# A four-layer graph network: 0/1 matrices kept in DRAM from layer 0 to layer 2, and two additions moved to other layers

## The chip, the cores and the metric

The kernel runs on one core of a Trainium2 chip. Times are device microseconds (us) of that core for one execution. The time before is 5064.37 us, the median of three runs (5048.0 to 5065.55).

Engines: PE (matrix multiplication; PEld is its weight load, which overlaps it), DVE (vector engine), ACT (scalar engine), POOL (GpSimd) and SP (SyncE, which only issues DMAs here). Each engine works through its own instructions in a fixed order. DMAs are issued from the queues of SP, ACT and POOL; the indirect ones, gathers and scatters with a row address per partition, are POOL's.

## The reference

50,000 nodes with 64 features, 25,000 directed edges that come sorted by their destination. Four layers, each with a normalisation and a rectification ahead of it and a residual sum behind it:

```python
h = maximum(layernorm(x), 0);  x = x + L0(h)    # mean of relu([h[src], h[dst]] @ W_msg + b_msg) over a node's edges,
                                                # then relu([h, mean] @ W_upd + b_upd)
h = maximum(layernorm(x), 0);  x = x + L1(h)    # (h + sum of h[src] * norm over a node's edges) @ W.T + b
h = maximum(layernorm(x), 0);  x = x + L2(h)    # attention over a node's edges (4 heads, 8 edge types),
                                                # y = layernorm(h + attention) * g1 + b1
                                                # L2 = layernorm(y + ffn(y)) * g2 + b2, ffn with gelu
h = maximum(layernorm(x), 0);  x = x + L3(h)    # expm(-t * B) h by a Taylor series of sparse products, B from edge_weight
```

So the x behind layer 2 is `x2 + layernorm(...) * g2 + b2`, where `x2` is the x behind layer 1, and the result is `x + L3(h)` with `L3(h) = h + POLY[1] * (B h) + ...`: the program folds the sub-steps of the series into one polynomial in B, `POLY`.

## The kernel before

**Tiling.** The nodes are taken in 49 items q of 1024 nodes, which lie as 8 blocks of 128 on the partitions (a tile [128, 8, 64]). The edges of an item fill up to 640 slots, 5 slot tiles of 128. As the edges are sorted, a node block j can touch only the slot tiles that the constant `BT[j]` names (first tile, number of tiles), and a slot tile i only the node blocks of `TB[i]`; `OHW` holds the column at which slot tile i begins in a row of 1920 columns.

**0/1 matrices.** A sum over the edges of a node, or the spreading of a node's row to its edge slots, is a matmul with a 0/1 matrix in bf16. There are two of an item. `noh` (node on the partition, slot on the free side; `node_hot`, L1883) is built by 8 DVE comparisons of 128 or 256 columns between the slots' keys, which `load_keys` (L1878) has broadcast to all partitions by a 160 KB DMA, and the node's own number. `soh` (slot on the partition, node on the free side; `slot_hot`, L1891) is built by 5 DVE comparisons of 256 to 512 columns, from a constant row and one key per partition. Layer 0 uses `noh` and `soh`, layer 1 `soh`, layer 2 both; layer 3's first product uses a `soh` with other keys (`skey`, the edges sorted by source). In layers 0 to 2 the keys, and so the matrices, are the same.

**Stages.** Each layer is a list of stages per item, run as a software pipeline: in each step every item in flight does its next stage, and a new item is begun (`Steps` and `pipeline`, L70 to L110). After every stage a hook, `lists_pace`, puts in some instructions of an independent job, building the lists of paths that layer 3's higher powers of B need; these are POOL scatters and gathers (`nmap`, `lgot`, `lrow`) and small DVE, PE and ACT work. Its rate is a number for each layer. From this program order a scheduler makes the fixed order of each engine; the number of buffers of a tile (`bufs`, otherwise 2) says when a buffer can be written again.

- *Layer 0* (L1977 to L2043): `fetch` (5 gathers `ga`, loads of `bt`, `cat`, `xt`, keys), `hots` (`node_hot`, `slot_hot`), `message` (PE with `noh`, then DVE and ACT), `sums` (PE with `soh`), `update`, `project` (stores `x1tab`, `g1tab`).
- *Layer 1* (L2046 to L2101): `fetch`, `scaled` (`slot_hot`, ACT scales the gathered rows), `sums` (L2070: PE into `po`, then DVE `x2 = x1 + po` at L2076, ACT's queue stores `x2tab` at L2077, then norm and rectification), `turn`, `product` (kv, q, h2 to DRAM).
- *Layer 2* (L2104 to L2398) has two pipelines. `up` is `fetch` (L2220: 5 gathers `kvg`, loads of `qt`, keys, `typ`), `hots` (L2231: `types` and `node_hot`), `logits` (L2236: PE `pv`, DVE `kk` and `vv`, store of `vv`, PE `pe` with `noh`). `down` is `fetch2` (L2305: loads of `vv`, `h2`), `message` (L2311: `slot_hot`, then `m3`), `sums` (PE with `soh`), `attend`, `turn`, `close` (loads `x2`), `product`, `finish` (L2370). The items go in batches of 13, 12, 12 and 12, with a softmax at the end of each: first `up` alone for 13 items, then `up` beside `down`, then `down` alone. `finish` multiplies by the norm and by g2 (L2380), adds b2 to `x2` (L2381), adds both (L2382), makes the next `h`, stores it (`h3tab`, L2385), adds it to x (L2386) and stores that (`xstab`, L2387).
- *Layer 3, first product B h* (L2483 to L2512): `fetch` (5 gathers `y` of `h3tab`, load of `xs`), `scaled` (`slot_hot`, ACT's scaling, a split in three bf16 parts), `sums` (PE `po`, ACT `f`, DVE `xs += POLY[1] * f`, stores). Then the higher powers, with final scatters that add to the output.

Of the kernel before, what the change touches and what calls it, by code (L numbers as in the profile page):

```python
# [22 lines left out]
F32 = mybir.dt.float32  # L23
# [35 lines left out]
TB = ((0, 3), (1, 3), (3, 3), (4, 4), (6, 2))  # L59
GRP = ((0, 1), (1, 2), (3, 1), (4, 2), (6, 2))  # L60
OHW = (0, 384, 768, 1152, 1664, 1920)

POLY = np.ones(1)
for _ in range(N_SUB):
# [901 lines left out]
def fast(ctx: ExitStack, tc: tile.TileContext, a: dict, out: bass.AP, flag: bass.AP):  # L966
# [25 lines left out]
    ktab = dram.tile([NQ, RW], F16, name="ktab")  # L992
    ttab = dram.tile([NQ, RW], F16, name="ttab")
    otab = dram.tile([NN, 1], I32, name="otab")
    vvtab = dram.tile([NQ * P, 5 * D], F32, name="vvtab")
    stab = dram.tile([P * TL, PW], I32, name="stab")
    nmap = dram.tile([NN, 1], I32, name="nmap")
# [3 lines left out]
    def nodes(tab, q):  # L1001
        return tab.rearrange("(p b) d -> p b d", p=P)[:, 8 * q:8 * q + 8, :]
# [879 lines left out]

    def node_hot(pool, s):  # L1883

        s.noh = pool.tile([P, 8, 2 * P], BF16, name="noh")
        for j in range(8):
            t0, n = BT[j]
            nc.vector.tensor_scalar(s.noh[:, j, :n * P], s.keys[:, t0 * P:(t0 + n) * P], pblk[:, j:j + 1], None,
                                    op0=OP.is_equal)

    def slot_hot(pool, keys, q):  # L1891
# [8 lines left out]
    def to_slots(po, s, tab, start=True):  # L1900

        for i in range(5):
            b0, nb = TB[i]
            for j in range(b0, b0 + nb):
                c = (i - BT[j][0]) * P
                for k in range(3):
                    nc.tensor.matmul(po[:, i, :], s.noh[:, j, c:c + P], tab[:, j, k * D:k * D + D],
                                     start=(start and j == b0 and k == 0), stop=(j == b0 + nb - 1 and k == 2))

    def to_sums(pa, oh, msg):  # L1910
# [66 lines left out]
    with tc.tile_pool(name="l0c", bufs=1) as cp, tc.tile_pool(name="l0", bufs=2) as pool, \  # L1977
            tc.tile_pool(name="pl0", bufs=1, space=PSUM) as ps:
        wupd = halves(None, a["L0_gnn_W_upd"][D:2 * D, :], a["L0_gnn_W_upd"][0:D, :], cp, "wupd")
        bupd = bias_rows(cp, row_bcast("L0_gnn_b_upd", pool=cp), "bupd")  # L1980
        w1t = cp.tile([P, D], F32, name="w1t")
        for h in range(2):
            nc.scalar.dma_start(w1t[h * D:(h + 1) * D, :], a["L1_gnn_WT"])

        def fetch(q, s):
            s.ga = pool.tile([P, 5, D], F32, name="ga", bufs=4)
            for i in range(5):
                gather(s.ga[:, i, :], atab, nrs[:, q, i:i + 1])
            s.bt = pool.tile([P, 8, BW], BF16, name="bt", bufs=4)
            nc.sync.dma_start(s.bt, nodes(btab, q))  # L1990
            s.cat = pool.tile([P, 2, 512], F32, name="cat", bufs=5)
            load_turned(s.cat, h0t, q)
            s.xt = pool.tile([P, 8, D], F32, name="xt", bufs=6)
            load_x(s.xt, q)
            load_keys(pool, q, s)

        def hots(q, s):
            node_hot(pool, s)
            s.soh = slot_hot(pool, key, q)

        def message(q, s):
            pe = ps.tile([P, 5, D], F32, name="pe", bufs=2)
            to_slots(pe, s, s.bt)
            z = pool.tile([P, 5, D], F32, name="z")
            nc.vector.tensor_add(z, s.ga, pe)
            m3 = pool.tile([P, 5, 3, D], F32, name="m3")
            for i in range(5):
                nc.scalar.activation(m3[:, i, 0, :], z[:, i, :], AF.Relu, scale=cinv[:, q, i:i + 1])  # L2008
            s.parts = split(m3)

        def sums(q, s):
            pa = ps.tile([P, 512], F32, name="pa")
            to_sums(pa, s.soh, s.parts)
            for h in range(2):
                r = slice(h * D, h * D + D)
                nc.scalar.activation(s.cat[r, h, :], pa[r, :], AF.Copy)

        def update(q, s):
            po = ps.tile([P, 8, D], F32, name="po")
            bias_in(po.rearrange("p b d -> p (b d)"), bupd)  # L2020
            for j in range(8):
                nc.tensor.matmul(po[:, j, :], s.cat[:, j // 4, j % 4 * P:j % 4 * P + P], wupd[j // 4],
                                 start=False, stop=(j == 7))
            s.x1 = pool.tile([P, 8, D], F32, name="x1", bufs=3)
            nc.vector.scalar_tensor_tensor(s.x1, po, 0.0, s.xt, op0=OP.max, op1=OP.add)
            s.h = pool.tile([P, 8, D], F32, name="h")
            norm_relu(pool, s.h, s.x1)

        def project(q, s):
            tr = turned(pool, ps, s.h, "pt")  # L2030
            g = pool.tile([P, 8, D], F32, name="g")
            for h in range(2):
                r = slice(h * D, h * D + D)
                pw = ps.tile([P, 4, D], F32, name=f"pw{h}")
                for i in range(4):
                    nc.tensor.matmul(pw[:, i, :], tr[r, i, :], w1t[r, :], start=True, stop=True)
                nc.vector.tensor_add(s.x1[:, h::2, :], s.x1[:, h::2, :], pw)
                nc.vector.tensor_mul(g[:, h::2, :], pw, over(disn[:, 8 * q + h:8 * q + 8:2], 4))
            nc.scalar.dma_start(nodes(x1tab, q), s.x1)
            nc.sync.dma_start(nodes(g1tab, q), g)  # L2040

        lists_pace.rate = 0.5
        pipeline(range(NQ), (fetch, hots, message, sums, update, project), lists_pace)  # L2043

    with tc.tile_pool(name="l1c", bufs=1) as cp, tc.tile_pool(name="l1", bufs=2) as pool, \
            tc.tile_pool(name="pl1", bufs=1, space=PSUM) as ps:
        b1l = bias_rows(cp, row_bcast("L1_gnn_b", pool=cp), "b1l")
        wkv = cp.tile([P, 4 * D], F32, name="wkv")  # L2050
        cen = ident_less_mean(cp)
        for h in range(2):
# [18 lines left out]
        def sums(q, s):  # L2071
            po = ps.tile([P, 8, D], F32, name="po")
            bias_in(po.rearrange("p b d -> p (b d)"), b1l)
            to_nodes(po, s.soh, s.parts, started=True)
            x2 = pool.tile([P, 8, D], F32, name="x2")
            nc.vector.tensor_add(x2, s.x1, po)  # L2076
            nc.scalar.dma_start(nodes(x2tab, q), x2)  # L2077
            s.h2 = pool.tile([P, 8, D], F32, name="h2")
            norm_relu(pool, s.h2, x2)

# [25 lines left out]
    with tc.tile_pool(name="l2c", bufs=1) as cp, tc.tile_pool(name="l2", bufs=2) as pool, \  # L2106
# [103 lines left out]
        pb = ps.tile([P, 1], F32, name="pe")  # L2210
        nc.tensor.matmul(pb, cen, zb[:, 0:1], start=True, stop=True)
        nc.vector.tensor_copy(zb[:, 1:2], pb)
        g2n, b2n = row_bcast("L2_gnn_ln2_g", pool=cp), row_bcast("L2_gnn_ln2_b", pool=cp)

        batches = [(0, 13), (13, 12), (25, 12), (37, 12)]
        batch_of = {q: k for k, (q0, n) in enumerate(batches) for q in range(q0, q0 + n)}
# [4 lines left out]
        def fetch(q, s):  # L2221
# [2 lines left out]
                gather(s.kv[:, i, :], kvtab, nrs[:, q, i:i + 1])  # L2224
            s.qt = pool.tile([P, 8, 3, D], BF16, name="qt", bufs=3)
            nc.sync.dma_start(s.qt.rearrange("p b k d -> p b (k d)"), nodes(qtab, q))
            load_keys(pool, q, s)
            s.typ = pool.tile([NE3, RW], F16, name="typ", bufs=2)
            nc.sync.dma_start(s.typ, ttab[q:q + 1, :].to_broadcast([NE3, RW]))

        def hots(q, s):  # L2231
            s.types = pool.tile([NE3, RW], BF16, name="types")
            nc.vector.tensor_scalar(s.types, s.typ, typei, None, op0=OP.is_equal)
            node_hot(pool, s)

        def logits(q, s):  # L2236
            k = batch_of[q]
# [17 lines left out]
            for i in range(5):  # L2255
                nc.tensor.matmul(pe[:, i, :], s.types[:, i * P:(i + 1) * P], etab[:, KW:], start=True, stop=False)
                b0, nb = TB[i]
                for j in range(b0, b0 + nb):
                    c = (i - BT[j][0]) * P
                    for k in range(3):  # L2260
                        nc.tensor.matmul(pe[:, i, :], s.noh[:, j, c:c + P], s.qt[:, j, k, :], start=False,  # L2261
                                         stop=(j == b0 + nb - 1 and k == 2))
            nc.vector.tensor_mul(kk, kk, pe)
            nc.vector.tensor_reduce(lg, kk.rearrange("p t (h d) -> p t h d", h=NH), AX.X, OP.add)
# [40 lines left out]
        def fetch2(q, s):  # L2305
            s.vv = pool.tile([P, 5, D], F32, name="vv2", bufs=3)
            nc.sync.dma_start(s.vv.rearrange("p t d -> p (t d)"), vvtab[P * q:P * q + P, :])
            s.h2 = pool.tile([P, 8, D], F32, name="h2", bufs=3)
            nc.sync.dma_start(s.h2, nodes(h2tab, q))

        def message(q, s):  # L2311
            k = batch_of[q]
            c = (q - batches[k][0]) * NH
            s.soh = slot_hot(pool, key, q)
            m3 = pool.tile([P, 5, 3, D], F32, name="m3")
            nc.vector.tensor_mul(
                m3[:, :, 0, :].rearrange("p t (h d) -> p t h d", h=NH), s.vv.rearrange("p t (h d) -> p t h d", h=NH),
# [52 lines left out]
        def finish(q, s):  # L2370
# [7 lines left out]
            nc.vector.tensor_mul(halved(x3), po,  # L2378
                                 r.rearrange("p (i h) -> p i h", h=2)[:, :, :, None].to_broadcast([P, 4, 2, D]))
            nc.vector.tensor_mul(x3, x3, along(g2n, 8))  # L2380
            nc.vector.tensor_add(s.x2, s.x2, along(b2n, 8))  # L2381
            nc.vector.tensor_add(x3, x3, s.x2)  # L2382
            h = pool.tile([P, 8, D], F32, name="h")
            norm_relu(pool, h, x3)
            nc.scalar.dma_start(nodes(h3tab, q), h)  # L2385
            nc.vector.tensor_add(x3, x3, h)  # L2386
            nc.scalar.dma_start(nodes(xstab, q), x3)  # L2387

        lists_pace.rate = 1.2
# [93 lines left out]
    with tc.tile_pool(name="mps", bufs=1, space=PSUM) as mps, tc.tile_pool(name="l3", bufs=2) as pool, tc.tile_pool(name="pl3", bufs=2, space=PSUM) as ps:  # L2483
        def fetch(q, s):
# [2 lines left out]
                gather(s.y[:, i, :], h3tab, sptr[:, 5 * q + i:5 * q + i + 1])  # L2487
            s.xs = pool.tile([P, 8, D], F32, name="xs", bufs=4)
            nc.sync.dma_start(s.xs, nodes(xstab, q))

        def scaled(q, s):
            s.soh = slot_hot(pool, skey.rearrange("p (q i) -> p q i", i=5), q)
            y3 = pool.tile([P, 5, 3, D], F32, name="y3")
            for i in range(5):
                nc.scalar.activation(y3[:, i, 0, :], s.y[:, i, :], AF.Copy, scale=swgt[:, 5 * q + i:5 * q + i + 1])
# [129 lines left out]
```

## Time and profile before

| | us |
|---|---|
| median of three runs | 5064.37 |
| the profiled execution | 5101.1 |
| its span, first to last record | 5099.3 |
| PE busy | 2720.2 (53%) |
| DVE busy | 2666.0 (52%) |
| POOL busy | 2207.3 (43%) |
| PEld busy | 1907.3 (37%) |
| ACT busy | 1256.2 (25%) |
| layer 0, from 1096 to 1905 | 809 |
| layer 1, from 1905 to 2610 | 705 |
| layer 2, from 2610 to 3981 | 1371 |
| layer 3's first product, from 3981 to 4420 | 439 |
| the higher powers, to the end | 679 |

Before layer 0 stand the sorting of the edges and the tables, 1096 us in all. The stage borders are read from the first and last records of each layer's tiles; stages overlap a little, as the next layer's first items begin before the last ones of the layer before are done.

How to read the lines that follow in the prediction. A row of the windows view is a stretch of the span: its length, busy us and instructions of PE, PEld, DVE, ACT and POOL, the mean granted clock of PE as a share of full speed, the busy share of the 16 DMA engines, and GB/s. A row of the waits view says: engine, tile and line that waited, what for, us in total, times, longest. A row of the groups view says: line, engine, operation, out<-in with shapes and types, count | busy us, mean ns of one | idle us of the engine just before them, and what ended it ("issue" is no wait that the profile shows, "remote" one whose end it can't place). A row of the timeline is start, length, engine, line, instruction, and in brackets the idle time before it. A row of the DMA queues is packets, MB, and the time of the packets as a share of 16 engines' span; q1 holds SP's, q10 ACT's transfers.

### The profile page before, as it was taken

The numbers are of one execution on the slowest core, as the hardware profiler recorded it, in microseconds if no ns is written. First come the engines' busy times: TensorE is split into PE (matmuls) and PEld (weight loads), VectorE is DVE, ScalarE is ACT, GpSimd is POOL, SyncE is SP. The second block draws the span as 40 slices with busy tenths as digits, with TensorE's granted clock in tenths as the row PEclk, the third lists the DMA queues.
The fourth block names the chain that finished last, engine by engine and source line by source line (L and its number), as shares of the span: only waits on it lengthen the run. The fifth ranks groups of instructions, "written<-read, shape, count | busy, mean of one in ns | idle before, by whom it ended". The sixth has DMA issues, their size and how long they took to land. (4 is left out here: it accounts for less than half of the span.)

```text
span 5099.3 us, 60799 instructions
## 1 busy us (share of the span) xinstructions
PE 2720.2 (53%) x20407; PEld 1907.3 (37%) x20407; DVE 2666.0 (52%) x8592; ACT 1256.2 (25%) x2922; POOL 2207.3 (43%) x2095
## 2 busy tenths in 40 slices
PE   8217304738888984245545763655667354433500
PEld 3002203636667763134433432333333243333400
DVE  9317406866667774245565674566688453312300
ACT  0000103612222223235530332333448222100000
POOL 0770571023323315644425254554320465546786
PEclk9555555556556656567765766767778675555555
DMA  1000214735434424245554222223222344312222
GB/s 38 4 1 2 56 27 130 219 87 140 108 99 110 125 72 110 70 117 167 167 147 118 84 69 72 83 73 88 77 71 82 80 103 119 91 18 41 36 17 12
DMA packets 521881, 424.60 MB, mean 83 GB/s; under 512 B 293924, under 2 KB 400579, under 8 KB 521301
## 3 DMA queue, kind: packets, MB, share of 16 engines
q1 hardware_dynamic: 347236, 241.04, 17.7%
q10 hardware_dynamic: 86976, 126.75, 7.1%
q0 software_dynamic: 87344, 52.82, 6.8%
q8 instruction: 163, 2.67, 0.2%
q14 instruction: 162, 1.32, 0.1%
HBM read 204.24 MB, written 218.11 MB: 83 GB/s over the span
## 5 line engine op out<-in xcount | busy, mean ns | idle before, releaser
L1005 POOL DMA_INDIRECT ga<-atab,nrs x245 | 254.3, 1038 | 773.2 <-DVE bupd_w L1106 304.0
L1936 PEld LDWEIGHTS <-soh 128*128 128x128 bf16 x4410 | 242.5, 120 | 597.7 <-issue 576.0
L1005 POOL DMA_INDIRECT kvg<-kvtab,nrs x245 | 251.4, 1026 | 485.2 <-DVE vv L2251 334.0
L1005 POOL DMA_INDIRECT gt<-g1tab,nrs x245 | 243.6, 994 | 372.5 <-ACT g L2068 213.4
L1005 POOL DMA_INDIRECT y<-h3tab,sptr x245 | 252.2, 1029 | 333.3 <-DVE soh L1896 165.1
L2558 POOL DMA_INDIRECT out<-y,lnode x183 | 283.3, 1548 | 141.3 <-DVE y L2544 75.0
L1926 PE MATMUL pa<-soh,m 128*64 128x256 bf16 (+1 forms) x2646 | 286.1, 338 | 15.6 <-ACT m L2008 11.1
L1188 PE MATMUL pab<-wab,tr 64*128 64x128 f32 x784 | 150.3, 437 | 264.8 <-issue 220.9
L1010 POOL DMA_INDIRECT stab<-raw,pf x196 | 194.6, 993 | 213.4 <-DVE pf L1393 154.0
L1005 POOL DMA_INDIRECT raw<-otab,nrd x196 | 189.9, 969 | 192.3 <-DVE bad L1151 132.5
L2532 DVE TENSOR_SCALAR s<-kr,lkey,lw 128x128 f32<-128x128 f32 x305 | 101.6, 402 | 312.9 <-issue 129.5
L1936 PE MATMUL po<-y,soh 128*128 128x64 bf16 x2205 | 147.3, 225 | 211.5 <-issue 129.4
L1936 PE MATMUL po<-g,soh 128*128 128x64 bf16 x2205 | 142.5, 229 | 208.5 <-DVE ln_v L1130 88.6
L1188 PEld LDWEIGHTS pab<-wab,tr 64*128 64x128 f32 x784 | 136.3, 324 | 283.8 <-issue 223.3
L2537 PE MATMUL pu<-y,s 128*128 128x64 f32 x366 | 109.2, 416 | 245.9 <-issue 99.4
L1130 DVE TENSOR_REDUCE ln_v<-ln_sq 128x8 f32<-128x512 f32 x294 | 196.7, 679 | 81.1 <-ACT ln_sq L1143 55.1
L2261 PE MATMUL pe<-qt,noh 128*128 128x64 bf16 x2205 | 168.9, 225 | 98.5 <-issue 94.1
L1374 DVE SCALAR_TENSOR_TENSOR junk<-rowi,f_sblk,pz 128x392 f32<-128x392 f32 x196 | 114.5, 619 | 196.5 <-remote 118.5
L1926 PEld LDWEIGHTS <-m 128*64 128x64 bf16 x2646 | 183.1, 143 | 91.0 <-issue 45.1
L1896 DVE TENSOR_SCALAR soh<-it,key 128x384 bf16<-128x384 f16 (+2 forms) x735 | 203.8, 316 | 7.9 <-PE pa L1926 3.5
L1005 POOL DMA_INDIRECT lgot<-nmap,ldst x183 | 179.1, 979 | 63.1 <-issue 53.6
L2261 PEld LDWEIGHTS <-noh 128*128 128x128 bf16 x2205 | 117.5, 115 | 212.6 <-issue 127.3
(571 smaller groups left out, 7621.4 us busy)
## 6 DMA issues: line engine op xcount, KB each, us to landing
kvtab<-kv SPq DMA_DIRECT2D x49, 512.0 KB
xt<-in_x SPq DMA_DIRECT2D x96, 256.0 KB
btab<-bt ACTq DMA_DIRECT2D x49, 384.0 KB
bt<-btab SPq DMA_DIRECT2D x49, 384.0 KB
qtab<-qt ACTq DMA_DIRECT2D x49, 384.0 KB
qt<-qtab SPq DMA_DIRECT2D x49, 384.0 KB
keys<-ktab SPq DMA_DIRECT2D x98, 160.0 KB
h0t<-tr ACTq DMA_DIRECT2D x98, 128.0 KB
```

Source lines behind the costliest of these rows:

```text
L1005: return nc.gpsimd.indirect_dma_start(out=dst, out_offset=None, in_=tab[:, :], in_offset=IndirectOffsetOnAxis(ap=idx, axis=0))
L1010: return nc.gpsimd.indirect_dma_start(out=tab[:, :], out_offset=IndirectOffsetOnAxis(ap=idx, axis=0), in_=src, in_offset=None, bounds_chec ...
L1130: nc.vector.tensor_reduce(v, sq, AX.X, OP.add)
L1188: nc.tensor.matmul(pab[:, i, :], s.tr[r, i, :], wab[r, :], start=True, stop=True)
L1374: nc.vector.scalar_tensor_tensor(junk, rowi[:, :BK], sblk[:, t:t + 1], pz, op0=OP.is_equal, op1=OP.mult, accum_out=slot[:, t:t + 1])
L1896: nc.vector.tensor_scalar(oh[:, OHW[i]:OHW[i + 1]], it16[:, b0 * P:(b0 + n) * P], keys[:, q, i:i + 1], None, op0=OP.is_equal)
L1926: nc.tensor.matmul(o, l, r, start=first, stop=last)
L1936: nc.tensor.matmul(po[:, j, :], oh[:, c:c + P], msg[:, i, k, :], start=(not started and i == t0 and k == 0), stop=(end and (not started or ...
L2261: nc.tensor.matmul(pe[:, i, :], s.noh[:, j, c:c + P], s.qt[:, j, k, :], start=False, stop=(j == b0 + nb - 1 and k == 2))
L2532: nc.vector.tensor_scalar(d[:, i, :], kr[:, i, :], s.key[:, t:t + 1], s.w[:, t:t + 1], op0=OP.is_equal, op1=OP.mult)
L2537: nc.tensor.matmul(pu[:, i, :], s0[:, i, :], y[:, t, :], start=True, stop=not s.onwards(t))
L2558: st = nc.gpsimd.indirect_dma_start(out=out[:, :], out_offset=IndirectOffsetOnAxis(ap=s.node[:, t:t + 1], axis=0), in_=sums[k][:, t, :], i ...
```

## The change: two matrices stored and loaded, two additions moved

- A new table in DRAM, `ohtab`, takes both matrices of every item: 128 rows of 2 x 1920 bf16. `noh` is laid out anew, from 8 x 256 columns to 1920 without gaps (`NOH` gives the offsets). Layer 0's `message` stores `noh` from SP's queue and `soh` from ACT's, 480 KB each.
- Layer 2's `fetch` loads `noh` (3 buffers, SP) where it loaded the keys, and `hots` no longer builds it. `fetch2` loads `soh` (3 buffers, SP), and `message` no longer builds it.
- The addition of b2 moves from layer 2's `finish` to layer 1's `sums`: `x2tab` now holds `x2 + b2`, in a tile of its own, `x2b`; the norm there still reads `x2`. The row b2 is loaded in layer 1's setup.
- The addition `x + h` moves from layer 2's `finish` to layer 3's `scaled`, whose `fetch` loads h from `h3tab` (256 KB, 3 buffers, SP).

```diff
@@ node_hot
-        s.noh = pool.tile([P, 8, 2 * P], BF16, name="noh")
+        s.noh = pool.tile([P, OHW[-1]], BF16, name="noh")
...
-            nc.vector.tensor_scalar(s.noh[:, j, :n * P], s.keys[:, t0 * P:(t0 + n) * P], pblk[:, j:j + 1], None,
+            nc.vector.tensor_scalar(s.noh[:, NOH[j]:NOH[j] + n * P], s.keys[:, t0 * P:(t0 + n) * P], pblk[:, j:j + 1], None,
@@ layer 0, message
+            nc.sync.dma_start(ohtab[P * q:P * q + P, 0, :], s.noh)
+            nc.scalar.dma_start(ohtab[P * q:P * q + P, 1, :], s.soh)
@@ layer 1, setup and sums
+        b2n = row_bcast("L2_gnn_ln2_b", pool=cp)
...
             nc.vector.tensor_add(x2, s.x1, po)
-            nc.scalar.dma_start(nodes(x2tab, q), x2)
+            x2b = pool.tile([P, 8, D], F32, name="x2b")
+            nc.vector.tensor_add(x2b, x2, along(b2n, 8))
+            nc.scalar.dma_start(nodes(x2tab, q), x2b)
@@ layer 2, setup, fetch and hots
-        g2n, b2n = row_bcast("L2_gnn_ln2_g", pool=cp), row_bcast("L2_gnn_ln2_b", pool=cp)
+        g2n = row_bcast("L2_gnn_ln2_g", pool=cp)
...
-            load_keys(pool, q, s)
+            s.noh = pool.tile([P, OHW[-1]], BF16, name="noh", bufs=3)
+            nc.sync.dma_start(s.noh, ohtab[P * q:P * q + P, 0, :])
...
             nc.vector.tensor_scalar(s.types, s.typ, typei, None, op0=OP.is_equal)
-            node_hot(pool, s)
@@ layer 2, fetch2 and message
+            s.soh = pool.tile([P, OHW[-1]], BF16, name="soh", bufs=3)
+            nc.sync.dma_start(s.soh, ohtab[P * q:P * q + P, 1, :])
...
-            s.soh = slot_hot(pool, key, q)
@@ layer 2, finish
-            nc.vector.tensor_add(s.x2, s.x2, along(b2n, 8))
             nc.vector.tensor_add(x3, x3, s.x2)
...
             nc.scalar.dma_start(nodes(h3tab, q), h)
-            nc.vector.tensor_add(x3, x3, h)
             nc.scalar.dma_start(nodes(xstab, q), x3)
@@ layer 3, fetch and scaled
+            s.h = pool.tile([P, 8, D], F32, name="h", bufs=3)
+            nc.sync.dma_start(s.h, nodes(h3tab, q))
...
             s.soh = slot_hot(pool, skey.rearrange("p (q i) -> p q i", i=5), q)
+            nc.vector.tensor_add(s.xs, s.xs, s.h)
```

The matmuls that read `noh` take its columns by `NOH[j]`; their number and shapes stay.

More of the change, by code (lines that the diff above doesn't have):

```diff
@@ L61 @@
 OHW = (0, 384, 768, 1152, 1664, 1920)
+NOH = (0, 128, 384, 640, 896, 1152, 1408, 1664)
 POLY = np.ones(1)
@@ L994, in fast @@
     otab = dram.tile([NN, 1], I32, name="otab")
+    ohtab = dram.tile([NQ * P, 2, OHW[-1]], BF16, name="ohtab")
     vvtab = dram.tile([NQ * P, 5 * D], F32, name="vvtab")
@@ L1904, in to_slots @@
             for j in range(b0, b0 + nb):
-                c = (i - BT[j][0]) * P
+                c = NOH[j] + (i - BT[j][0]) * P
                 for k in range(3):
-                    nc.tensor.matmul(po[:, i, :], s.noh[:, j, c:c + P], tab[:, j, k * D:k * D + D],
+                    nc.tensor.matmul(po[:, i, :], s.noh[:, c:c + P], tab[:, j, k * D:k * D + D],
                                      start=(start and j == b0 and k == 0), stop=(j == b0 + nb - 1 and k == 2))
@@ L2258, in logits @@
                 for j in range(b0, b0 + nb):
-                    c = (i - BT[j][0]) * P
+                    c = NOH[j] + (i - BT[j][0]) * P
                     for k in range(3):
-                        nc.tensor.matmul(pe[:, i, :], s.noh[:, j, c:c + P], s.qt[:, j, k, :], start=False,
+                        nc.tensor.matmul(pe[:, i, :], s.noh[:, c:c + P], s.qt[:, j, k, :], start=False,
                                          stop=(j == b0 + nb - 1 and k == 2))
```

## The prediction

> **What bounds the kernel now.** I read the windows of each stage first, then the waits of the stages, then the groups of DVE instructions, then timelines of single items, and the DMA queues. The chain that ended last is empty here (every share 0%), so the bound is read stage by stage.
>
> ```profile
> core 0: us, PE busy (x) PEld busy (x) DVE busy (x) ACT busy (x) POOL busy (x), PEclk, DMA share, GB/s
> 1096.00:1905.00 809.00, 684.07 (x5967) 556.20 (x5967) 552.40 (x2106) 193.44 (x491) 255.61 (x247) 0.59 0.43 111
> 1905.00:2610.00 705.00, 332.46 (x3292) 261.87 (x3292) 342.93 (x857) 294.58 (x883) 336.63 (x342) 0.69 0.47 131
> 2610.00:2830.00 220.00, 116.05 (x1202) 83.23 (x1203) 114.90 (x477) 17.64 (x54) 102.15 (x103) 0.50 0.41 116
> 2830.00:3640.00 810.00, 473.05 (x3327) 274.88 (x3323) 480.15 (x1631) 261.15 (x445) 376.90 (x361) 0.69 0.27 78
> 3640.00:3981.00 341.00, 229.79 (x1224) 121.15 (x1225) 278.17 (x729) 203.44 (x314) 41.06 (x36) 0.79 0.24 75
> 3981.00:4420.00 439.00, 204.91 (x2373) 159.65 (x2373) 186.43 (x488) 106.85 (x334) 252.21 (x245) 0.62 0.44 107
> ```
>
> Row by row: layer 0; layer 1; layer 2 while only `up` runs; `up` with `down`; `down` alone; layer 3's first product. Layer 0 is PE's (684 of 809). Layer 1 belongs to no engine: a loop of waits. In layer 2, 1371 us, DVE is the busiest (873 in sum), and 278 of 341 us at its end. Two more windows, of 80 us in the middle of layer 2 and of its rhythm:
>
> ```profile
> 3140.00:3220.00 80.00, 61.67 (x462) 35.62 (x460) 67.20 (x208) 41.59 (x74) 27.43 (x26) 0.80 0.42 129
> ```
>
> There DVE is 84% busy. But the waits of 2830 to 3640 show something else too:
>
> ```profile
> POOL kvg L1005 <- DVE vv L2251: 248.9, 16, 31.6
> ...
> DVE kk L2263 <- remote: 92.1, 3, 76.2
> ...
> PE pe L2256 <- DVE kk L2263: 67.2, 2, 61.3
> ```
>
> A DVE wait of 76 us, and PE with it, falls where POOL issues list scatters and gathers back to back; all engines resume when it stops. Following DVE's gaps through the timeline, it stands idle for 251 us of this stage, 167 of them inside such POOL bursts (482 us long in sum). That time doesn't go with DVE work. So layer 2 is DVE's between the bursts and POOL's in them.
>
> The groups of DVE that the change touches:
>
> ```profile
> L1896 DVE TENSOR_SCALAR soh<-it,key 128x384 bf16<-128x384 f16 (+2 forms) x735 | 203.8, 316 | 7.9 <-PE pa L1926 3.5 <-remote 2.5 <-issue 1.9
> ...
> L1888 DVE TENSOR_SCALAR noh<-keys,pblk 128x256 bf16<-128x256 f16 (+1 forms) x784 | 177.0, 282 | 3.9 <-DMA keys<-ktab 3.9
> ...
> L2386 DVE TENSOR_TENSOR x<-x,h 128x512 f32<-128x512 f32 x49 | 33.7, 688 | 0.0
> L2076 DVE TENSOR_TENSOR x<-x,po 128x512 f32<-128x512 f32 x49 | 33.6, 686 | 214.0 <-remote 90.0 <-PE pp L2093 89.1 <-DMA qtab<-qt 15.2
> ...
> L2381 DVE TENSOR_TENSOR x<-x,b_L_gnn_ln_b 128x512 f32<-128x512 f32 x49 | 33.3, 679 | 4.9 <-DMA x<-x2tab 4.9
> ```
>
> The third field is mean ns. Neighbours overlap by about 80 ns in the records, so a removed instruction gives back its mean less 0.08.
>
> **Layer 2, DVE work removed.** Per item q: 8 noh builds x (0.282 - 0.08) = 1.62 us (a timeline at 2709.42 has them in 1.65); 5 soh builds x (0.316 - 0.08) = 1.18; two adds of 128x512, 2 x 0.60 = 1.20. Together 4.0, x 49 = 196 us. How much reaches the end:
> - `up` alone, 13 items: the rhythm is POOL's, five gathers an item, and after every ten a wait for `vv`:
>
> ```profile
> 2709.42 0.23 DVE L1888 TENSOR_SCALAR noh<-keys,pblk 128x128 bf16<-128x128 f16 x1
> ...
> 2709.70 1.46 DVE L1888 TENSOR_SCALAR noh<-keys,pblk 128x256 bf16<-128x256 f16 x7
> ...
> 2711.07 0.34 DVE L2250 TENSOR_TENSOR kk<-kvg,pv 128x192 f32<-128x192 f32 x1
> ...
> 2712.34 0.95 POOL L1005 DMA_INDIRECT kvg<-kvtab,nrs  x1 [6.22 <-DVE vv L2251]
> ```
>
>   Without noh, `kk` may start at 2709.95, where PE's `pv` ends: 1.1 us per pair, 6.5 pairs, **-7**. Late next: the gather's landing.
> - `up` with `down`: 36 x 1.62 + 30 x 2.38 (soh and adds) = 130 us. DVE isn't idle in 567 of the stage's 818 us; 315 of those lie in bursts, 252 between. I count the share between (44%, 57 us) in full and half of the rest (36): **-90**, rounded.
> - `down` alone, 19 items: 19 x 2.38 = 45. DVE was 82% busy, ACT 60%, with 64 table loads of 1.283 us. ACT's chain is next, so two thirds: **-30**.
>
> **Layer 2, loads added.** Two loads of 480 KB an item, one 160 KB `keys` load less. Both stand on SP beside `qt` and `h2`; noh's buffer is freed by the same `pe` of three items before as `qt`'s, soh's by `sums`, before `h2`'s. So the new waits hold back nothing on SP that wasn't held, and each load has a step of at least 12 us. Cost:
>
> ```profile
> q1 hardware_dynamic: 347236, 241.04, 17.7%
> q10 hardware_dynamic: 86976, 126.75, 7.1%
> ```
>
> SP's queue moves 241.04 MB in 17.7% of 5099 us = 267 GB/s while busy, so 480 KB take 1.84 us. No row shows a transfer of just this size. **0**; if the cover is gone, up to 2 x 1.84 - 0.6 for `keys` = 3.1 us an item.
>
> **Two rules against it.** The Trainium skill, "DMA: Bandwidth & Descriptors", section "Anatomy of one DMA", gives 2.0 us plus bytes/436e3 for one transfer: an estimate of 3.1 us for 480 KB, two of them 6.3 us against 2.8 us of builds, so loading would lose if the transfer stood on the path. At a lead of 12 us neither 1.84 nor 3.1 does; the sum is the same by both, the outer end isn't. Second, "VectorE: DVE Perf Modes", section on the errata, prices such a build at (58 + elements/4) cycles of 0.96 GHz: 0.95 us for eight noh (two of 128 elements, six of 256), 0.80 for five soh. Then 49 items lose 86 us of builds and 59 of adds = 145, not 196, and at my share (127/196) layer 2 gains 94, not 127, and the sum below is -39 instead of -72. The rows measure these same instructions, at 1.6 times the rule even after the overlap is taken off, so I take the rows.
>
> **Layer 0, stores added.** 2 x 480 KB an item on SP and ACT, +60 GB/s on 111. q10's rate is 350 GB/s, 1.4 us a store. SP's store waits for the same noh at which `keys` was issued before; behind it are `keys` for two items on. ACT's stands before `cat`, where ACT idles (215.9 us for `pa`). PE doesn't wait for either. **+5**, between 0 and +25 (0.5 us an item if `bt` or the gathers land later).
>
> **Layer 1, bias added.** The add stands between `x2` and the mean `ln_s`, in a loop of 11.4 us through `x2`, norm, `h` and PE's next `po`. The nearest row is L2381 itself: 0.60 x 49 = 29. A few items wait elsewhere ("remote 90.0"): **+25**, from +10 to +34 (its whole mean). The `x2tab` store waits 0.6 us longer on ACT, with `g`'s scaling behind it; POOL's `gt` waits for that `g` (213.4 us). The bias row's load moves with it into layer 1's setup, beside others there.
>
> **Layer 3, x + h.** The add stands on DVE between soh and the split that PE's `po` waits for; POOL's rhythm (5 gathers of 1.03 us and a wait for ACT's `y`) contains it: **+25**, from +15 to +30. The 256 KB load of h is issued ahead of `xs`'s. In layer 2 ACT's `xstab` store no longer waits for that add.
>
> **The sum.** -127 + 5 + 25 + 25 = -72, on 5101.1 us: 5029. The median of the three runs, 5064.4, lies 36.7 lower; the same 72 off it gives 4992, and I say 4990.
>
> **The rivals.** A measurement here tells 0.5%, 25 us, from no change.
> - *A, as summed, -45 to -120*: 0.55; 4945 to 5020.
> - *B, DVE is the bound all through layer 2*: for it, 84% busy at 3140 and 82% at the end. All 196 reach the end, and POOL's gathers (mean 1026 ns, median 947 by their list) gain 20 with fewer builds: -216 + 55 = -160, about 4905. Against it, the 76 us in which DVE was the one waiting. 0.15.
> - *C, bursts and PE set layer 2*: for it, the 248.9 us of POOL's waits. A third of 196, -65, +55 from layers 0, 1 and 3: -10, 5054. 0.17.
> - *D, slower: the loads delay the gathers.* `kvg` packets share the 16 DMA engines with the 480 KB loads, and POOL waits for `vv`, which needs them landed. If both loads stand ahead of a gather on each item, 3.1 x 49 = 152, so -72 + 152 = +80, 5144; the point from which it decides is 72/49 = 1.5 us an item. Against: the DMA share is 0.27 in the middle. For: 0.41 in `up` alone, 0.43 in layer 0, where it adds most. 0.13, counting milder forms near 5100.
>
> Faster by over 0.5% (below 5039): A, B and 0.02 of C, which has an edge there, 0.72. Within: the rest of C, 0.15. Slower (above 5090): D, 0.13. The range takes A, C and the upper half of B: 4905 to 5065.
>
> **What would show it.** Right: layer 2 (2610 to 3981) ends 100 to 150 us sooner, with DVE busy less by about 220 in records; layers 1 and 3 longer by 20 to 30 each; layer 0 by under 10; waits for noh and soh on DMA under 10 us. Wrong: DVE waits "DMA noh" or PE "DMA soh" of tens of us (D), a layer 2 shortened by under 80 with longer waits for "remote" (C), or by over 180 (B).

## The result, and the profile after

The changed kernel takes 4989.51 us (median of 4 runs, 4972.39 to 4996.51) against 5064.96 us before: a ratio of 0.9852, 95% interval 0.9818 to 0.9886, some 75 us less. The forecast was 4990. It came out so because its errors cancelled: the terms of its sum, looked at one by one, are mostly wrong, and this part of the document is about that.

The windows of the changed kernel by stage, in the columns of before (length, busy us of PE, PEld, DVE, ACT, POOL, granted clock, DMA share, GB/s). The rows are layer 0, layer 1, layer 2 as a whole, layer 3's first product and the higher powers:

```profile
1096.00:1890.00 794.00, 672.74 (x5967) 544.07 (x5967) 550.19 (x2095) 193.45 (x491) 253.96 (x246) 0.61 0.59 173
1890.00:2557.00 667.00, 324.29 (x3286) 255.30 (x3286) 375.15 (x903) 295.17 (x883) 358.52 (x342) 0.70 0.48 138
2557.00:3864.00 1307.00, 783.57 (x5752) 457.24 (x5753) 688.19 (x2110) 456.63 (x796) 504.39 (x499) 0.70 0.38 118
3864.00:4295.00 431.00, 187.40 (x2375) 152.28 (x2375) 212.37 (x536) 107.17 (x334) 282.44 (x245) 0.63 0.53 139
4295.00:4970.00 675.00, 183.01 (x794) 164.48 (x792) 107.30 (x310) 17.80 (x48) 457.29 (x366) 0.51 0.21 25
```

Two things don't fit the prediction. Layer 1 has more DVE work (375 us against 343) and is shorter, 667 instead of 705. Layer 2 lost 185 us of DVE work (873 to 688) and got only 64 shorter, 1371 to 1307: DVE went from 64% busy to 53%.

This profiled execution was 17 us under its median, and that of before 37 over its own, so the two traces differ by 129 us where the medians differ by 75. To compare stages I measure them between fixed instructions (from the last `x1` of layer 0 to the last `x2` of layer 1, from there to where the last `x3` of layer 2 is first written, from there to the last `xs`), and use a second profile of each program. One profile each, us:

| kernel | layer 1 | median between its items | layer 2 | layer 3, product | span |
|---|---|---|---|---|---|
| before | 706.1 | 11.40 | 1379.1 | 446.9 | 5099.3 |
| e5, as before but for noh's layout | 704.1 | 11.39 | 1377.4 | 445.6 | 5099.1 |
| after | 668.9 | 10.30 | 1314.7 | 438.0 | 4970.6 |
| e4, the changed kernel again | 677.6 | 10.45 | 1333.1 | 451.2 | 5025.1 |
| e1, matrices only | 709.6 | 11.40 | 1365.1 | 446.9 | 5088.9 |
| e2, b2 only | 678.3 | 10.44 | 1428.4 | 447.8 | 5121.9 |
| e3, x + h only | 709.2 | 11.39 | 1410.2 | 443.3 | 5123.7 |
| e10, matrices and b2 | 678.1 | 10.45 | 1345.6 | 445.1 | 5037.9 |
| e11, matrices and x + h | 709.5 | 11.39 | 1334.8 | 446.5 | 5062.7 |
| e6, layer 1 without gathers | 521.1 | 7.54 | 1386.2 | 445.2 | 4923.7 |
| e7, e6 and b2 | 537.7 | 8.23 | 1442.2 | 444.9 | 4994.4 |
| e8, before, no lists in layer 2 | 698.9 | 11.29 | 1086.8 | 541.9 | 5290.1 |
| e9, after, no lists in layer 2 | 667.5 | 10.33 | 1178.9 | 484.8 | 5113.2 |
| e12, x2 stored from SP | 699.6 | 12.93 | 1300.2 | 436.0 | 4988.1 |

Two profiles of the changed kernel differ by 18 us in layer 2 (1314.7 and 1333.1), 13 in layer 3 and 9 in layer 1; a smaller difference tells nothing by itself. From e5 to e4 the spans differ by 74 us: layer 0 -7, layer 1 -27, layer 2 -44, layer 3 +6, the rest -2.

The groups of DVE in the changed kernel show that it does what it says: 392 builds of noh instead of 784, 490 of soh instead of 735, and the two additions at their old price in their new places.

```profile
L1898 DVE TENSOR_SCALAR soh<-it,key 128x384 bf16<-128x384 f16 (+2 forms) x490 | 139.8, 321 | 3.7 <-PE pa L1928 3.5 <-issue 0.2
...
L1890 DVE TENSOR_SCALAR noh<-keys,pblk 128x256 bf16<-128x256 f16 (+1 forms) x392 | 91.9, 283 | 3.8 <-DMA keys<-ktab 3.8
...
L2502 DVE TENSOR_TENSOR xs<-xs,h 128x512 f32<-128x512 f32 x49 | 33.5, 685 | 0.4 <-DMA h<-h3tab 0.4
...
L2084 DVE TENSOR_TENSOR x2b<-x,b_L_gnn_ln_b 128x512 f32<-128x512 f32 x49 | 33.5, 684 | 0.0
```

### The profile page after: what moved, and what is told of

Read it like the earlier page. It is cut to its first block, busy times and chain, and to the rows that moved or that the text cites. A ratio compares the mean times of both kernels' runs of the same rounds, so it can differ in the third digit from the quotient of the medians.

```text
span 4970.6 us, 60481 instructions
## 1 busy us (share of the span) xinstructions
PE 2645.7 (53%) x20407; PEld 1857.5 (37%) x20407; DVE 2537.4 (51%) x7955; ACT 1231.6 (25%) x2905; POOL 2244.9 (45%) x2095
## 5 line engine op out<-in xcount | busy, mean ns | idle before, releaser
L1007 POOL DMA_INDIRECT kvg<-kvtab,nrs x245 | 239.0, 976 | 440.2 <-DVE vv L2259 215.6
L1007 POOL DMA_INDIRECT y<-h3tab,sptr x245 | 282.9, 1155 | 297.5 <-DVE soh L1898 170.5
L1938 PEld LDWEIGHTS <-soh 128*128 128x128 bf16 x4410 | 232.0, 119 | 489.8 <-issue 412.1
L1007 POOL DMA_INDIRECT gt<-g1tab,nrs x245 | 265.5, 1084 | 310.5 <-ACT g L2074 152.8
L1938 PE MATMUL po<-y,soh 128*128 128x64 bf16 x2205 | 132.1, 224 | 195.8 <-ACT y L2505 100.3
L1372 PE MATMUL pz<-pre,ident 98*128 98x392 f16 x196 | 94.4, 483 | 193.8 <-issue 95.8
L1133 ACT ACTIVATE ln_v<-ln_v,epsc 128x8 f32<-128x8 f32 x294 | 82.7, 296 | 456.4 <-DVE ln_v L1132 432.4
```

The lines of the kernel that those rows point to most:

```text
L1007: return nc.gpsimd.indirect_dma_start(out=dst, out_offset=None, in_=tab[:, :], in_offset=IndirectOffsetOnAxis(ap=idx, axis=0))
L1372: nc.tensor.matmul(pz, ident16[:HT2, u:u + 1].to_broadcast([HT2, P]), pre16[:, h, :], start=True, stop=False)
L1938: nc.tensor.matmul(po[:, j, :], oh[:, c:c + P], msg[:, i, k, :], start=(not started and i == t0 and k == 0), stop=(end and (not started or ...
```

## The parts one by one

The before of these runs was measured beside them on the same chip; it had medians from 5069 to 5116 us in these sessions, so ratios are compared, not times.

**e1, the matrices only.** Both additions are put back in layer 2:

```diff
+            nc.vector.tensor_add(s.x2, s.x2, along(b2n, 8))
             nc.vector.tensor_add(x3, x3, s.x2)
...
             nc.scalar.dma_start(nodes(h3tab, q), h)
+            nc.vector.tensor_add(x3, x3, h)
```

> Layer 0 stores both 0/1 matrices and layer 2 loads them; b2 is added in layer 2 and x + h formed in layer 2, as before. Theory P (the prediction's sum): 2.8 of the 4.0 us of DVE work an item go, so layer 2 gives 89 of its 127 us, layer 0 costs 5: -84 us on the time, 4980; layers 1 and 3 unchanged. Theory R (read from the two traces: layer 1 fell by 38 us although an instruction was added, layer 2 by only 67): the matrices give -40 to -60, layer 1's period stays at 11.4 us and layer 3's at about 9.

Measured: 5089.0 us against 5112.08, ratio 0.9945 (0.9926 to 0.9964), some 28 us less by the ratio. Layer 2 is 12 us shorter than e5's, which is within the spread. Theory R was nearer, and even it took too much.

**e2, b2's addition only.** Layer 2 builds its matrices as before, nothing is stored in layer 0:

```diff
-            nc.scalar.dma_start(nodes(x2tab, q), x2)
+            x2b = pool.tile([P, 8, D], F32, name="x2b")
+            nc.vector.tensor_add(x2b, x2, along(b2n, 8))
+            nc.scalar.dma_start(nodes(x2tab, q), x2b)
```

> Only b2's addition is moved from layer 2 to layer 1. Theory P: layer 1 +25, layer 2 -19: +6 us, no change that can be told. Theory R: with x2 + b2 in a tile of its own the fixed order of DVE in layer 1 is another (the split of the scaled rows stands ahead of the variance instead of behind it), and that, not the matrices, shortens layer 1's period from 11.4 to 10.3 us: layer 1 -30 to -40, time -30 to -50.

Measured: 5132.87 us, ratio 1.0040 (1.0024 to 1.0056). Layer 1 is 26 us shorter than e5's, as theory R has it. But layer 2, which has an instruction less, is 51 us longer, which neither theory had.

**e3, x + h only.** Here the matrices and b2 stay as before:

```diff
-            nc.vector.tensor_add(x3, x3, h)
...
+            nc.sync.dma_start(s.h, nodes(h3tab, q))
...
+            nc.vector.tensor_add(s.xs, s.xs, s.h)
```

> Only x + h is moved from layer 2 to layer 3. Theory P: layer 2 -19, layer 3 +25: +6 us. Theory R: layer 3's period falls or stays (its items came at 7.3 in the median instead of 9.1 us), so -10 to -25 us.

Measured: 5143.85 us, ratio 1.0066 (1.0046 to 1.0086), slower than both theories. Layer 3 is unchanged (443 against 446); layer 2 is 33 us longer.

**e4, the changed kernel again.**

> The changed kernel a second time, for the spread of its stages: 4970 to 5000 us. If the sum of the three parts run alone differs from this by over 20 us, the parts act on each other (theory P and theory R both expect them to add).

Measured: 5026.9 us, which is above the 5000 expected, but beside a before of 5112.08: ratio 0.9827 (0.9802 to 0.9852). The three ratios of the parts multiply to 1.005. So the parts don't add: apart they give nothing, together 1.7%.

**e5, nothing moved.** The control: the changed kernel with all parts undone but noh's layout.

> Only noh's columns are laid out anew; all else as before. Both theories: no change that can be told, and stages within the spread of two profiles of one kernel: layer 1's items at 11.4 us, layer 2 some 1380 us from layer 1's last item to its own. If layer 2 differs by over 40 us from that, the spread of layer 2 is larger than what the parts did to it one by one.

Measured: 5119.49 us, ratio 1.0003 (0.9992 to 1.0015), and every stage within 4 us of before's. So layer 2's +51 and +33 in e2 and e3 are no spread.

**e10 and e11, the matrices with one addition each.**

> The changed kernel with x + h left in layer 2: matrices stored and loaded, b2 moved. Theory W (with the builds gone, each addition taken out of layer 2 pays, about 25 us each, the difference of layer 2's 1365 us in e1 and 1315 to 1333 in the changed kernel halved): layer 2 at 1330 to 1350 us, layer 1 at its short period of 10.3. Theory A (layer 2's length follows how the scheduler happens to place POOL's list runs, and no sum of parts gives it): layer 2 may lie anywhere from 1310 to 1430 us, and e10 and e11 can't both be read as the halves of one difference.

> The changed kernel with b2 left in layer 2: matrices stored and loaded, x + h moved. Theory W: layer 2 at 1330 to 1350 us, layer 1 at its long period of 11.4, so some 30 us slower than e10. Theory A: as at e10.

Measured: 0.9850 (0.9830 to 0.9871) and 0.9891 (0.9870 to 0.9912). Both layers 2, 1345.6 and 1334.8, lie in theory W's range, and layer 1 is short in e10 and long in e11. So the first addition taken out of layer 2 costs 33 to 51 us while the builds are there, and gains 20 to 30 once they are gone (the second one then gains 2 to 31, by the two profiles of the changed kernel, which is within the spread). Seen from the other side, the matrices gain 12 us with both additions in layer 2, 83 with b2 out (1428.4 to 1345.6) and 75 with x + h out (1410.2 to 1334.8). Theory A isn't refuted by this: e2 and e3 are what it allows, and theory W says nothing of them. e10 is as fast as the changed kernel within the intervals.

## Layer 1: POOL's gathers set its rhythm

The timeline of one item of before in layer 1 (start, length, engine, line, instruction, idle time):

```profile
2299.05 0.69 DVE L2076 TENSOR_TENSOR x<-x,po 128x512 f32<-128x512 f32 x1 [3.76 <-PE pp L2093]
...
2300.17 0.35 ACT L2068 ACTIVATE g<-gt,dise 128x64 f32<-128x64 f32 x1 [4.19 <-DVE soh L1896]
...
2301.73 0.63 ACT L1143 ACTIVATE ln_sq<-ln_xc 128x512 f32<-128x512 f32 x1 [1.21 <-DVE ln_xc L1141]
...
2302.26 0.57 ACT L2068 ACTIVATE g<-gt,dise 128x64 f32<-128x64 f32 x2
...
2303.10 1.19 POOL L1005 DMA_INDIRECT gt<-g1tab,nrs  x1 [5.19 <-ACT g L2068]
...
2305.77 1.58 PE L1936 MATMUL po<-g,soh 128*128 128x64 bf16 x27
...
2307.27 2.10 PE L2093 MATMUL pp<-wkv,tr 64*128 64x256 f32 x16
2308.35 0.95 POOL L1005 DMA_INDIRECT gt<-g1tab,nrs  x1 [0.31 <-issue]
...
2310.41 0.69 DVE L2076 TENSOR_TENSOR x<-x,po 128x512 f32<-128x512 f32 x1 [3.75 <-PE pp L2093]
```

and the same of the changed kernel:

```profile
2289.76 0.69 DVE L2082 TENSOR_TENSOR x<-x,po 128x512 f32<-128x512 f32 x1 [2.56 <-PE pp L2101]
...
2291.68 0.82 ACT L2074 ACTIVATE g<-gt,dise 128x64 f32<-128x64 f32 x3 [2.83 <-DVE x2b L2084]
...
2292.78 1.04 POOL L1007 DMA_INDIRECT gt<-g1tab,nrs  x1 [3.50 <-ACT g L2074]
...
2293.04 0.63 ACT L1145 ACTIVATE ln_sq<-ln_xc 128x512 f32<-128x512 f32 x1 [0.53 <-DVE ln_xc L1143]
...
2298.62 0.94 POOL L1007 DMA_INDIRECT gt<-g1tab,nrs  x1 [0.30 <-issue]
...
2300.06 0.69 DVE L2082 TENSOR_TENSOR x<-x,po 128x512 f32<-128x512 f32 x1 [2.56 <-remote]
```

Before, ACT scales one tile of gathered rows, waits for the norm's `ln_xc`, squares it, and only then scales two more; POOL's next five gathers wait for those (5.19 us). With b2's addition the scheduler made another order: ACT scales all three ahead of the square, so POOL starts 3.02 us after `x2` instead of 4.05. The next `x2` follows the end of POOL's fifth gather: by 1.11 to 1.28 us in each of the last 27 items with gathers before, by some 0.5 in the changed kernel (0.6 in e4). The medians of these items sum to the period: from `x2` to POOL's start, POOL's run, and from its end to the next `x2` make 4.05 + 6.19 + 1.16 = 11.40 before and 3.02 + 6.80 + 0.47 = 10.29 after. The run itself got 0.6 us longer and the wait behind it 0.7 shorter, so about the earlier start is left as the gain, and the added 0.6 us of DVE lies in the shade of POOL's run. A hint that it is POOL: the last three items, for which nothing is left to gather, came every 7.5 us before. (In the changed kernel they came every 8.2 to 8.4 us in one profile and every 7.6 to 8.3 in the other.)

**e6 and e7, layer 1 without its gathers**, once with before's order and once with b2 moved:

```diff
-            for i in range(5):
-                gather(s.gt[:, i, :], g1tab, nrs[:, q, i:i + 1])
+            nc.sync.dma_start(s.gt, nodes(g1tab, q)[:, :5, :])
```

> The kernel before, but layer 1's 245 gathers by POOL are left out: each item's 160 KB come by one plain load on SP's queue, of other rows, so the values differ. DVE's order in layer 1 is that of before. Theory G (POOL's run of five gathers holds back what PE signals, so x2 comes 1.1 us after the run's end and POOL sets the period): layer 1's items come at about 7.5 us, as the last four do now, for which no gather is left. Theory O (DVE's order itself, the split behind the variance, sets 11.4): near 11 us still.

> As e6, with b2's addition moved to layer 1 (and the order of DVE that goes with it). Theory G: the added instruction costs its 0.6 to 0.8 us an item where no gather runs: 8.2 to 8.4 us an item against e6's 7.5, and layer 1 is some 30 us longer than e6's. Theory O: the new order is the faster one here too: about 1 us an item under e6.

Measured: items at 7.54 and 8.23 us in the median, layer 1 521.1 and 537.7. That speaks against theory O and for theory G's rhythm without gathers; of the addition's cost that theory G named, about half came. The periods alternate in both (mostly 7.5 and 8.1 to 8.4 in e6, 7.7 and 8.3 to 8.5 in e7), so their medians mislead: the mean of the last 39 items is 7.79 and 8.05 us, and the layer is 17 us longer, not 30. Some 100 us of each without a gather, by windows (e6, then e7):

```profile
2250.00:2350.00 100.00, 73.37 (x864) 58.17 (x860) 85.95 (x209) 75.65 (x234) 0.00 (x0) 0.88 0.83 243
```

```profile
2250.00:2350.00 100.00, 71.52 (x798) 56.90 (x796) 91.19 (x215) 73.22 (x225) 0.00 (x0) 0.85 0.79 237
```

DVE is 86 and 91% busy there, the busiest engine, and of the added instruction's 0.6 us about 0.3 an item shows. With the gathers nothing of it does. (e7's layer 2 is 56 us longer than e6's, the +51 of e2 a second time.)

What the gathers delay can be seen in e6, where `x2` follows PE's last matmul of `po` at once:

```profile
2308.08 1.64 PE L1936 MATMUL po<-g,soh 128*128 128x64 bf16 x27
...
2309.76 0.69 DVE L2075 TENSOR_TENSOR x<-x,po 128x512 f32<-128x512 f32 x1 [0.49 <-PE po L1936]
```

Before, `po` ends at 2307.35 by its record, and `x2` starts 3.1 us later. The semaphore events in the trace tell whether PE was late or only its signals: PE signals once for `po` and four times for the `pp` behind it. In e6 these five events spread over 2 to 3 us. Before, they come at 2310.39, 2310.45, 2310.51, 2310.57 and 2310.63, and in the same way, within 0.24 us, in each of 28 items. PE can't have done in 0.24 us what takes it 2 to 3 us in e6, so its work was done, and its signals came late. What held them is not shown.

**e12, the store of x2 moved to SP's queue.** In the changed kernel ACT's scaling stands behind the store that waits for `x2b`; with the store elsewhere it could start sooner.

```diff
-            nc.scalar.dma_start(nodes(x2tab, q), x2b)
+            nc.sync.dma_start(nodes(x2tab, q), x2b)
```

> The changed kernel with one queue changed: layer 1's store of x2 + b2 is issued by SP instead of ACT, so ACT's scaling of the gathered rows no longer stands behind a store that waits for x2b. Theory G (POOL's run of five gathers starts when ACT has read the older rows, and x2 comes half a microsecond after the run's end): ACT frees the rows earlier in the period, the run starts earlier, and layer 1's items come at 8.5 to 9.5 us instead of 10.3 to 10.45, so 35 to 80 us less in layer 1; layer 2 may shift by 20 either way with its order: 4950 to 5000 against the changed kernel's 5027 on such a chip. If the chain through x2 and the norm itself sets 10.4, layer 1 stays as it is.

Measured: ratio 0.9860 (0.9835 to 0.9885), no better than the changed kernel. Layer 1 went the other way, 699.6 us: the scheduler's order is again another, and items come in pairs, 13.9 and 8.3 us apart, 11.1 in the mean. Layer 2 is 15 to 33 us shorter than in the changed kernel. A miss, as 8.5 to 9.5 us were expected: the scaling did wait behind that store (the 2.83 us for `x2b` above), but an edit that frees it doesn't keep the rest of the order.

## Layer 2: the list runs

The waits of the changed kernel in layer 2 (engine, tile, what for: us, times, longest):

```profile
POOL kvg L1007 <- DVE vv L2259: 215.6, 24, 24.7
...
DVE kk L2271 <- remote: 140.4, 13, 34.1
...
ACT sums L2338 <- remote: 103.0, 5, 49.7
DVE m L2325 <- remote: 84.7, 5, 49.0
```

Two of these rows in the kernel before, from 2610 to 3981:

```profile
DVE kk L2263 <- remote: 120.6, 6, 76.2
...
ACT sums L2329 <- remote: 63.9, 8, 21.7
```

So the waits for "remote" grew, but they are only a part of what DVE's removed work turned into. From the last `x2` to the last `x3` DVE stood idle for 501 us before, and for 622 in the changed kernel (640 in e4). Of these 121 us more, 41 lie in gaps of over 8 us and 78 in gaps of 1 to 8 us (46 and 91 in e4); of the latter, those that end with PE grew from 86 us to 132 (114 in e4). What the long gaps are shows best in the longest one of before:

```profile
3066.49 0.10 PEld L2256 LDWEIGHTS <-types 24*128 24x128 bf16 x1 [1.92 <-issue]
3067.45 0.94 POOL L1005 DMA_INDIRECT lgot<-nmap,ldst  x1 [0.30 <-issue]
...
3118.69 0.95 POOL L1005 DMA_INDIRECT lgot<-nmap,ldst  x1 [0.30 <-issue]
3126.84 0.32 SPq L2226 DMA_DIRECT2D qt<-qtab  x1
3126.84 0.49 DVE L2263 TENSOR_TENSOR kk<-kk,pe 128x320 f32<-128x320 f32 x1 [76.21 <-remote]
...
3127.39 0.20 PE L2256 MATMUL pe<-etab,types 24*128 24x64 bf16 x1 [61.33 <-DVE kk L2263]
```

PE's record of the matmuls that `kk` and SP's `qt` wait for ends before 3066. Both start in the same instant, 3126.84, 7.2 us after the last indirect DMA of POOL's run. Between lies nothing but POOL's DMAs, one every 1.25 us. Either PE's matmuls ran later than recorded, or what they signal came late, as in layer 1; here it is a single signal, at 3126.82, and the trace can't tell which. Not every run stops the other engines: in the one from 2984 to 3054 us (42 list scatters and 5 gathers) DVE is busy for 48 of 70 us. Over the nine runs of 13 and more DMAs in before's layer 2, 387 us in sum, DVE is busy 43% of the time and PE 39%; outside of POOL's runs it is 76 and 69%. DVE's gaps of over 8 us in layer 2 sum to 243 us before (255 in e5), 304 in e1, 320 in e2, 283 in e3 and 283 after (289 in e4).

**e8 and e9, the lists taken out of layer 2**, from the kernel before and from the changed one:

```diff
-        lists_pace.rate = 1.2
+        lists_pace.rate = 0.0
```

> The kernel before with the lists' rate in layer 2 set from 1.2 to 0: their scatters and gathers come in layer 3 instead, so layer 2 holds POOL's 245 gathers only. Theory G (POOL's runs of list DMAs stop the other engines): layer 2, some 1378 us from layer 1's last item to its own last, falls by 200 us or more, its DVE gaps over 8 us shrink from some 240 us to under 100, and what is left is DVE's. Theory D (DVE's work is the bound of layer 2 with the lists too): layer 2 falls by under 80. The time as a whole may rise, as the lists lose their cover.

> The changed kernel with the same rate of 0 in layer 2. Theory G: without the runs the 4 us of DVE work an item reach the end at the prediction's 65% or more: layer 2 is 120 to 190 us shorter than e8's, where with the runs it was 44 to 62 shorter. Theory D2 (something else than the runs eats the gain, such as the 96 MB of stores and loads): the difference stays at 40 to 70.

Measured, e8: layer 2 is 1086.8 us, 291 less than e5's. Its window, without the edges:

```profile
2598.00:3677.00 1079.00, 775.96 (x5641) 461.99 (x5642) 804.60 (x2294) 462.87 (x797) 251.62 (x245) 0.73 0.36 105
```

POOL's instructions fall from 498 to 245, and the long gaps to 56 us. So the lists cost layer 2 1.15 us for each of 253 DMAs, nearly the 1.25 us at which POOL issues them: work that was thought to lie beside the other engines' is paid almost in full. Not all of it need be the DMAs' doing, as the lists' small work on DVE left layer 2 with them (878 us of DVE in layer 2 before, 807 in e8). That is theory G's first half. (The time as a whole is 4% longer, as layer 3 pays more for them still.)

e9 doesn't show the second half. The scheduler drew lists from layer 3 into the end of layer 2 there (129 list DMAs between 3300 and 3730 us), so 1178.9 us is no measure. Up to the 37th item of `down`, ahead of those, it is 24 us sooner than e8 (891.6 against 915.4 from layer 1's end), and the 37th item of `up` 75 us sooner. That is less than theory G's 120 to 190 for the whole, in a part where PE is busy 403 us of 500. How much of DVE's saving a layer 2 without runs would pass on stays open.

Why an addition less costs 33 to 51 us (e2, e3) isn't settled either. What can be seen is the fixed order of POOL: with b2 taken out, 33 list gathers stand in one run with 20 `kvg` gathers behind it, where before they were 30, 5 `kvg`, 10, then 20 `kvg`; in the changed kernel those list gathers are cut into runs of 14 and fewer (though 33 list scatters behind them stand in one). The gaps go with it (320 us in e2 against 243). But e3 speaks against the length of that one run: there the list gathers stand in runs of 27 and 13, where before they were 30 and 10, and layer 2 is 33 us longer all the same. That the order of the runs is the cause was argued, not tried; no kernel with before's instructions and another order was run.

## Why the prediction was right, and where it was not

- **Up alone, -7.** Right. The 13th `kk` comes 164.0 and 165.4 us behind layer 1's end in the two profiles of the changed kernel, 171.9 and 171.6 without the change: -6 to -8. (In e1 and e10, with the same matrices, it comes at 168.5 and 168.4, so -3.)
- **Up with down, -90.** Wrong. To the 30th item of `down` the gain is 1118 - 1070 = 48 and 1117 - 1090 = 27 us, the -7 included, so 20 to 41. The step that failed is "I count the share between (44%) in full and half of the rest": not even the 57 us counted in full came through, and the parts' runs (e1's -12, e2's +51 for layer 2) show that its length follows no sum of DVE work. The share was also read too high: "isn't idle in 567" takes every short gap for work, while the stage's own row has DVE busy for 480 of 810 us.
- **Down alone, -30.** Too much by half: from the 30th item to the last it is 261 and 260 us without the change, 245 and 243 with it, so -16 to -17, or 0.9 us an item of the 2.38. Some 11 to 13 of it lie in the first six items, beside the last list runs, of 4 to 6 DMAs. In the 13 items behind them it is 0.35 us an item, and there no run of lists explains why so little came through. The windows of 110 us, before and after:

```profile
3790.00:3900.00 110.00, 84.26 (x436) 43.67 (x435) 94.36 (x231) 79.05 (x116) 4.74 (x4) 0.85 0.27 86
```

```profile
3680.00:3790.00 110.00, 80.16 (x479) 42.54 (x477) 77.39 (x166) 74.55 (x116) 4.33 (x4) 0.92 0.42 129
```

  DVE fell from 86 to 70% busy: being busy for 86% didn't make DVE the bound. The step that failed is "ACT's chain is next, so two thirds": little over one third came through. What the bound is was not tried; by the look of the timeline it is a chain from engine to engine, ACT's table loads in it.
- **Layer 2 in sum, -127.** -44 to -64. The removed work was sized well (DVE's busy time fell by 185 us, against 196 in the sum and 220 named for the records); the share of it that reaches the end was not. This was rival C's figure for layer 2 (-65), and the sign named for it came: a layer 2 shortened by under 80, with longer waits for "remote". The sign of being right, 100 to 150 us, did not. C failed as a whole with the +55 that it took over for layers 0, 1 and 3.
- **The loads in layer 2, 0, and the stores in layer 0, +5.** Right. Layer 0 went from 111 to 173 GB/s and did not get longer; from the first `x1` to the last it lasts 736 and 745 us in the changed kernel and 750 to 752 in e1, e10 and e11, which have both stores, and 743 to 752 in before, e2, e3 and e5, which have none. Rival D had no case: the only wait put down to one of the two loads in layer 2 is 0.6 us long, and e6 moved 243 GB/s at a DMA share of 0.83 and was the fastest layer 1.
- **Layer 1, +25.** Wrong in sign, 26 to 37 us shorter. The step was "the add stands between x2 and the mean, in a loop of 11.4 us through x2, norm, h and PE's next po". The loop runs through POOL's gathers; the 3.1 us from the recorded end of PE's last `po` to `x2` were the place to look. Where no gather runs, about half of the step's 0.6 us shows.
- **Layer 3, +25.** -9 to +6, so nothing that can be told; e3 and e11, which have the addition there, are at 443 and 447 us, those without at 445 to 448. "POOL's rhythm contains it" is the step that failed. By analogy with layer 1 the addition lies beside POOL's run of gathers; no run tested that. (The load of h stands behind that of `xs`, not ahead of it; waiting for it cost DVE 0.4 us in all.)
- **The rule or the rows.** Neither choice decided anything. The transfers stayed hidden, as both prices had it (the fit that the prediction takes from the Trainium skill, "DMA: Bandwidth & Descriptors", section "Anatomy of one DMA", is given there for transfers that GpSimd issues; these loads are SP's). And of the removed builds and additions so little came through that 196 or 145 us of them can't be told apart by the time. The second rule was also taken too narrowly. An item's noh is one build of 128 elements and seven of 256, as the prediction's own lines show, so the rule makes 0.98 us of it, not 0.95. And the same section of "VectorE: DVE Perf Modes" in the Trainium skill says that its row under-predicts and that the measured fixed term is about 150 cycles, not 58: with that an estimate is 1.75 us for the eight noh and 1.28 for the five soh, near the 1.62 and 1.18 that the trace's rows gave.

So of -127 + 5 + 25 + 25 = -72 the runs put about -44 - 7 - 27 + 6 - 2 = -74 in its place (e4 against e5): 83 us too much in layer 2, and 52, 19 and 12 us too little in layers 1, 3 and 0.

## What to carry to other kernels

An engine that is 85% busy isn't yet the bound: before counting its saved work, find the instruction that ends the loop's longest unexplained wait and see what ended just ahead of it, in every item (here POOL's last gather, by 1.1 to 1.3 us). Where a period alternates, compare means or whole stages, not medians. Where a scheduler makes the order, one instruction more or less re-makes the order of every engine, and that can weigh more than the instruction: price an edit as a new order, by what it puts ahead of the waits that count, and test parts in pairs, as they need not add. A total that comes out as forecast proves none of its terms.

## What the hardware showed that I had not expected

While POOL issues indirect DMAs back to back, one each 1.25 us, PE's signals can reach the other engines late: in layer 1 five of them, for 2 to 3 us of work, come within 0.24 us, 1.1 us after each run's end, and a DVE wait of 76 us ends 7.2 us after a run. Other work goes on in part: DVE is busy 43% of the time in the long runs of layer 2 and 76% outside of them. 253 list DMAs taken out of layer 2, with 71 us of DVE work that goes with them, made it 291 us shorter. And the same kernel had medians from 5065 to 5116 us in different sessions, 5116 and 5070 of them on what the record numbers as the same chip, so only runs beside each other can be compared.
